# Row products with two weight matrices: from plain matmuls on row tiles to Strassen's scheme on pairs of row tiles

## The chip, the cores and the metric

The kernel runs on one core of a Trainium2 chip. The metric is device time in microseconds (us) of one execution, the median of several runs. A core has five engines with instruction streams of their own: TensorE (PE, matrix products; PEld its weight loads), VectorE (DVE), ScalarE (ACT), GpSimd (POOL) and SyncE (SP, which here only issues transfers). [...] 

## What is computed

Two layers of a graph network on 3327 nodes with D = 512 features, in float32:

```
# layer 0: attention; ahead of it a layer norm
h = relu(layernorm(x))
q, k, v = h @ Wq.T + bq, h @ Wk.T + bk, h @ Wv.T + bv
x1 = x + softmax(q @ k.T / sqrt(512) + adj + adj) @ v
# layer 1: normalised graph convolution
h1 = relu(layernorm(x1))
A2 = adj + I
dscale = diagonal(A2) ** -0.5
temp = A2 @ h1 @ W.T
out = x1 + relu((dscale * A2 * dscale) @ temp)      # dscale by rows and by columns
```

The kernel doesn't form v. With p for the exponentials it multiplies the square matrix with the rows of h first and with the weights after: (p @ h) @ Wv.T, divided by the sum of the row of p; the bias is then added to each row, since a row of the softmax sums to one. The same order is used in layer 1. So three times a square matrix of 26 x 26 row tiles (26 tiles of 128 rows, padded) meets rows of 512 numbers: p with h (g = 0), the adjacency with h1 (g = 1), and the adjacency with the rows that layer 1 made by the weights (g = 2). After g = 0 and after g = 1 each of the 26 row tiles is multiplied with a 512 x 512 weight matrix. These 52 row products are what is changed.

## The kernel before

**Prelude** (up to about 120 us of the trace): products of the weights, the layer norm and ReLU of x (`h_transposed`), transposes, and `project_q`. **Scores** (to about 640 us): `Pair` makes scores and their exponentials, and writes them to memory in the seven combinations that Strassen's scheme needs.

**Steps.** The three large products are done by Strassen's scheme with the 2 x 2 blocks of the matrix. There are 294 steps, numbered by `number_of(g, r, s, t)`: g is the product (0 to 2), r one of seven block products in the order p5, p1, p6, p7, p2, p3, p4, s one of two strips of columns (896 and 768 wide, so that a matmul has 448 or 384), and t runs over 0 to 5 and None. A step with t of 0 to 5 applies Strassen's scheme once more inside: `four_sums` (L170 to L172) makes three combinations of the left-hand tile on VectorE, `Right.make` four differences of the right-hand rows (L176 to L179), and seven matmuls (L772) add into seven PSUM banks (`ROLE`: p1 in bank 0, and so on). The step None has four matmuls (L764) for the thirteenth tile; its product p8 lies in bank 3. After it `gather` makes the strip's result from the banks: a copy of p1 on ScalarE (L796) and eight operations on VectorE (L797 to L805). `settle` (L820 to L827) adds it into the results of the 2 x 2 blocks: nothing for p5 and p1, six operations for p7, two for the others. The sums of step k + 2 are made behind the matmuls of step k, and its transfers are issued three steps ahead.

**Row products.** `times_weights` (L860) multiplies one row tile with a weight matrix by four matmuls of 512 columns into bank 3, the same that p8 and the transposes at the end use. In g = 0 `attend` then scales and adds x on VectorE (L872), adds the bias (L873), stores the tile (L874) and starts the norm (`norm`: L190, L192, L194 on VectorE, a power on GpSimd at L196, and nb on VectorE at L200); `attended`, one step later, applies the ReLU on ScalarE (L879) and stores the row (L880). x is loaded by ScalarE's queue one step ahead (L867). In g = 1 `temp` scales on ScalarE (L888) and stores. `rows` places one row tile beside a step, from the step (g, 5, 1, 2), where the first rows are complete, to the first strips of g + 1; a row tile's matmuls come behind those of its step. `Job` (L851, L854) makes sums of the adjacency for layer 1, in steps of g = 0 and g = 1.

**Order.** `run(k)` writes out the order in which each engine gets its work, and it is kept as written: the transfers of step k + 3, the matmuls of step k, the gather if t is None, the sums of step k + 2, settle, and then what `between` holds for this step (loads and blocks of the right-hand side, jobs, row products). In the third product `finish` (L913) transposes, applies ReLU, adds x1 and stores.

Of the kernel before, what the change touches and what calls it, by code (L numbers as in the profile page):

```python
# [10 lines left out]
F32 = mybir.dt.float32  # L11
# [29 lines left out]
Q = tuple(n * P // 2 for n in HT)  # L41


@with_exitstack
def graph_layers_kernel(
# [117 lines left out]
    totd = dram.tile([1, NP], F32, name="totd")  # L163
    x1d = [dram.tile([P, D], F32, name=f"x1d{i}") for i in range(NT)]
# [3 lines left out]
    def four_sums(o, g):  # L168

        nc.vector.tensor_add(o[:, 0:2], g[:, 0:4:3], g[:, 1:2].to_broadcast([P, 2, g.shape[-1]]))  # L170
        nc.vector.tensor_add(o[:, 2], o[:, 1], g[:, 0])  # L171
        nc.vector.tensor_add(o[:, 3], o[:, 2], g[:, 2])  # L172
# [93 lines left out]
    x_ring = ring(*((mid, k) for k in range(10, 15)), (half, 13), (half, 14))  # L266
    n_ring = ring(*((mid, k) for k in range(4)))

    def load_x(i, queue=nc.sync):
        xt = x_ring([P, D], "xt")  # L270
        queue.dma_start(xt, x[i * P : (i + 1) * P])
        return xt
# [16 lines left out]
    nc.sync.dma_start(bq_sb, bq)  # L289
    M = blocks(range(4, 8), "M")  # L290
# [3 lines left out]
    zero = half(12, [P, P], "zero")  # L294
# [16 lines left out]
    def h_transposed(k):  # L311

        a, n = PACKS[k]
        for _, i in (o for o in order if o[0] == k):
# [4 lines left out]
            nc.gpsimd.dma_start(rowd[0][i], ht)  # L319
# [11 lines left out]
        nc.vector.tensor_add(hp[k][:, 6], hp[k][:, 1], hp[k][:, 4])  # L331

    def project_q(k):
# [5 lines left out]
        def chain(o):  # L339
# [12 lines left out]
            def last():  # L352
                if o == 1:
                    for j in range(4):
                        y, z = divmod(j, 2)
                        i = (y * HALF + a) * P
                        nc.gpsimd.dma_start(qd[:, 2 * z : 2 * z + 2, i : i + w], qs[j][:, :, :w])
# [13 lines left out]
    for k, then in itertools.zip_longest(TURN, TURN[1:]):  # L371
        if then is not None:
            h_transposed(then)
        project_q(k)

# [30 lines left out]
    def adjacency(s, q, t):  # L406
# [3 lines left out]
        for k in range(2):  # L410
            r0, c0 = (k * HALF + t) * P, STRIPS[s] * P
            src = adjT[r0 : r0 + P, c0 : c0 + 2 * H[s]].rearrange("p (y w) -> p y w", y=2)
            nc.sync.dma_start(g[k], src[:, :, c : c + wd])
        return g

    class Pair:
# [11 lines left out]
        def sum_of_adjacency(self, m):  # L428
# [7 lines left out]
            for k, y in parts:  # L436
                d = diagonal(o, (k * HALF + t) * P, STRIPS[s] * P + y * H[s] + self.c)
# [138 lines left out]
    def seven():  # L576
        return {r: bank(ROLE[r], r) for r in ("p1", "p6", "p7", "p5", "p2", "p3", "p4")}
# [33 lines left out]
    rs = const.tile([P, NT], F32, name="rs")  # L611

    def weights(src):

        w = [half(k, [P, 2, D], "w") for k in (12, 13)]
        for c in range(DC):
            nc.sync.dma_start(w[c // 2][:, c % 2], src[c * P : (c + 1) * P])
        return [w[c // 2][:, c % 2] for c in range(DC)]
# [4 lines left out]
    bvs = []  # L623

    def prepare():
        wv_w1.append(weights(wvT))
        bvs.append(half(11, [P, D], "bv_sb"))
        nc.sync.dma_start(bvs[0], bass.AP(tensor=bv.tensor, offset=bv.offset, ap=[[0, P], [1, D]]))
# [4 lines left out]
    def prepared():  # L633
        nc.vector.reciprocal(rs, tot)
        nc.vector.tensor_scalar(dg, dg, 1.0, None, op0=ALU.add)
        nc.gpsimd.tensor_tensor(sd, dg, mh, op=ALU.pow)

    wv_w1 = []

    def other_weights():  # L640
        wv_w1.append(weights(w1T))
# [17 lines left out]
    r_ring = ring(*((half, k) for k in (4, 5, 6, 7)))  # L659
# [11 lines left out]
    job_ring = ring(*spare[2:], (half, 14))  # L671
    h_ring = ring(*spare[:2])
    ts_ring = ring(*spare[:3])
# [5 lines left out]
    def left(g, s, what, t):  # L679
# [4 lines left out]
        for k, j in enumerate(js):  # L684
# [7 lines left out]
            r0, c0 = (z * HALF + j) * P, STRIPS[s] * P + y * H[s]  # L692
# [6 lines left out]
    class Right:  # L699
# [9 lines left out]
        def rows(self, dst, h, z):  # L709

            for k, i in enumerate(self.its):
                src = rowd[self.g][h * HALF + i]
# [18 lines left out]
        def make(self):  # L731
            own, r = self.own, self.r
            if r == "p5":
                nc.vector.tensor_sub(own, self.two[:, :, 0:E], self.two[:, :, E:D])
            if r == "p6":
                nc.vector.tensor_add(own, own, self.two[:, :, 0:E])
                nc.vector.tensor_sub(own, own, self.two[:, :, E:D])
                nc.gpsimd.dma_start(self.t2[:, 0 : 2 * self.n], self.b[:, 0 : 2 * self.n])
            if r in ("p7", "p4"):
                nc.vector.tensor_sub(own, own, self.one)  # L740
            if self.n == 2:
                for _ in four_differences([self.b[:, k] for k in range(8)]):
                    pass

    class Step:
# [8 lines left out]
        def sums(self):  # L754
# [3 lines left out]
            four_sums(self.o, self.a.rearrange("p k y w -> p (k y) w"))  # L758

        def multiply(self, ps):  # L760
# [6 lines left out]
            o = self.o  # L767
            for r, i, m in (
                ("p1", 0, a[:, 0, 0]), ("p6", 5, o[:, 2]), ("p7", 6, o[:, 0]), ("p5", 4, o[:, 1]),
                ("p2", 2, a[:, 1, 0]), ("p3", 3, o[:, 3]), ("p4", 7, a[:, 1, 1]),  # L770
            ):
# [5 lines left out]
    def gather(ct, r, s, ps, last):  # L777

        hw, qw = H[s], Q[s]

        def region(y, z):
            return [ct[y][2 * z + k] for k in range(2)]

        place = {"p5": (1, 1), "p1": (0, 0)}.get(r)
        if place:
            to = region(*place)
        else:
            to = [cts["to"][k][:, :hw] for k in range(2)]
        p = {k: v[:, :qw] for k, v in ps.items()}
        lo, hi = slice(0, qw), slice(qw, hw)  # L790
        r11, r12, r21, r22 = region(0, 0), region(0, 1), region(1, 0), region(1, 1)
        into = r21 if last else None


        c11, c12, c21, c22 = to[0][:, lo], to[1][:, lo], to[0][:, hi], to[1][:, hi]
        nc.scalar.copy(c11, p["p1"])  # L796
        nc.vector.tensor_sub(c22, p["p6"], c11)  # L797
        nc.vector.tensor_add(c21, c22, p["p7"])
        nc.vector.tensor_sub(c12, c22, p["p5"])
        nc.vector.tensor_sub(c22, c21, p["p5"])  # L800
        if into is None:
# [4 lines left out]
        else:  # L806

            o11, o12, o21, o22 = (t[k][:, w] for t, k, w in ((into, 0, lo), (into, 1, lo), (into, 0, hi), (into, 1, hi)))
            nc.vector.tensor_add(o11, o11, c11)
            nc.vector.tensor_sub(o12, o12, c12)  # L810
            nc.vector.tensor_add(o21, o21, c21)
            nc.vector.tensor_add(o22, o22, c22)
            flags.append(nc.values_load(bad, min_val=0, max_val=1))
            for o, k in ((o11, "p2"), (o12, "p3"), (o21, "p4"), (o22, "p8")):
                nc.vector.tensor_add(o, o, p[k])

        def settle():
            for k in range(2):
                if r == "p6":
                    nc.vector.tensor_sub(r12[k], to[k], r11[k])  # L820
                elif r == "p7":
                    nc.vector.tensor_add(r21[k], to[k], r12[k])  # L822
                    nc.vector.tensor_sub(r12[k], r22[k], r12[k])  # L823
                    nc.vector.tensor_sub(r22[k], r21[k], r22[k])  # L824
                elif not place and into is None:
                    t = {"p2": r11, "p3": r12, "p4": r21}[r]
                    nc.vector.tensor_add(t[k], t[k], to[k])  # L827

        return settle
# [6 lines left out]
    class Job:  # L836
# [5 lines left out]
        def load(self):  # L842
            s, j, w = self.s, self.j, H[self.s]
            self.a, self.b = (job_ring([P, H[0]], "job")[:, :w] for _ in range(2))
            r0, c0 = (self.k * HALF + j) * P, STRIPS[s] * P
# [10 lines left out]
    def times_weights(i, w):  # L856
        s, y, k = where(i)
        ps = bank(ROLE["p8"], "p8")
        for d in range(DC):
            nc.tensor.matmul(ps, cts[s][y][d][:, k * P : (k + 1) * P], w[d], start=d == 0, stop=d == DC - 1)  # L860
        return ps

    xts = {}

    def attend_load(i):
        xts[i] = view(2, 1).rearrange("p a w -> p (a w)")[:, len(xts) % 3 * D :][:, :D]
        nc.scalar.dma_start(xts[i], x[i * P : (i + 1) * P])  # L867

    def attend(i):

        xt, ps = xts[i], times_weights(i, wv_w1[0])
        nc.vector.scalar_tensor_tensor(xt, ps, rs[:, i : i + 1], xt, op0=ALU.mult, op1=ALU.add)  # L872
        nc.vector.tensor_add(xt, xt, bvs[0])  # L873
        nc.gpsimd.dma_start(x1d[i], xt)  # L874
        normed[i] = norm(xt)

    def attended(i):
        h1 = h_ring([P, D], "h1")
        nc.scalar.activation(h1, xts[i], AF.Relu, bias=normed[i][1](), scale=normed[i][0])  # L879
        nc.gpsimd.dma_start(rowd[1][i], h1)  # L880

    normed = {}

    def temp(i):

        ps = times_weights(i, wv_w1[1])
        ts = ts_ring([P, D], "ts")
        nc.scalar.mul(ts, ps, sd[:, i : i + 1])  # L888
        nc.gpsimd.dma_start(rowd[2][i], ts)
# [62 lines left out]
    def rows(g, k, i, *z):  # L952

        if g == 0:
            at(k - 1, attend_load, i)
            at(k, attend, i)
            at(k + 1, attended, i)
        elif g == 1:
            at(k, temp, i)
        else:  # L960
            at(k - 1, finish_load, i, *z)
            at(k, finish, i, *z)


    for g in range(2):
        for t, i in {2: 0, 3: 1, 4: 2, 5: 3}.items():
            rows(g, number_of(g, 5, 1, t), i)
        for t, i in enumerate((4, 5, 6, 14, 15, 16)):
            rows(g, number_of(g, 6, 0, t), i)
        for t, its in {1: (7,), 2: (8, 9), 3: (10,), 4: (11, 12), 5: (13,)}.items():  # L970
            for i in its:
                rows(g, number_of(g, 6, 1, t), i)
# [431 lines left out]
```

## Time and profile before

| what | us |
|---|---|
| median of 3 runs (lowest, highest) | 2236.4 (2235.24, 2238.02) |
| the profiled execution | 2233.93 |
| its span, from the first to the last instruction | 2231.7 |
| TensorE busy | 2185.5 |
| VectorE busy | 1623.9 |
| ScalarE, GpSimd busy | 230.7, 354.8 |
| matmuls of steps: L772, L764 | 1255.5, 124.2 |
| matmuls of scores: L449, three kinds | 309.2, 162.6, 81.1 |
| row products: L860, two kinds of operands (272 and 144 records) | 125.5, 67.6 |

The program's matmuls of float32 stand in the trace as two records each, so that a row product has eight records of 512 columns. A matmul's end is modelled, so a record's duration is longer than the distance to the next one; distances between starts are what counts for TensorE. In the lists of waits a line says which engine and line waited for which, with the sum, the number of times and the longest. In a timeline each line has the start, the duration, the engine, the line, the operation with output and input, and in brackets how long the engine had been idle and what released it.

### The profile page before, as it was taken

How to read it: one execution, taken by the hardware profiler on the slowest of the kernel's cores; microseconds unless marked ns; L12 is line 12 of the kernel's file. 1: busy time of each engine (PE TensorE's matmuls, PEld its weight loads, DVE VectorE, ACT ScalarE, POOL GpSimd, SP SyncE). 2: the span in 40 equal slices, each digit the busy share in tenths (PEclk: the TensorE clock that was granted, in tenths of full speed). 3: DMA queues.
4: the chain of work that ended last, by engine and by line, in shares of the span. 5: the costliest groups of instructions: out<-in, count | busy, mean ns of one | idle time of the engine just before them, and what ended most of it. 6: DMA issues, size and time to landing. Idle time of an engine off the chain costs nothing. (4 is left out here: it accounts for less than half of the span.)

```text
span 2231.7 us, 21005 instructions
## 1 busy us (share of the span) xinstructions
PE 2185.5 (98%) x6268; PEld 1169.3 (52%) x6268; DVE 1623.9 (73%) x3092; ACT 230.7 (10%) x336; POOL 354.8 (16%) x551
## 2 busy tenths in 40 slices
PE   9999999999999999999999999999999999999997
PEld 5555555455545555555444555555544555555554
DVE  6369888788878788877777778886543547777676
ACT  5321121112110000000010000000000000000011
POOL 4223333333321000001221110000000000000001
PEclk9999999999999999999999999999999999999998
DMA  7568888888969998888787899876645458765695
GB/s 253 204 210 309 294 296 287 302 283 305 350 215 329 327 366 283 280 300 272 258 293 240 298 337 355 280 280 202 217 126 195 141 174 299 243 187 185 210 307 172
DMA packets 246682, 583.68 MB, mean 262 GB/s; under 512 B 34768, under 2 KB 106270, under 8 KB 246558
## 3 DMA queue, kind: packets, MB, share of 16 engines
q1 hardware_dynamic: 192270, 399.28, 54.2%
q0 software_dynamic: 44928, 167.49, 19.7%
q10 hardware_dynamic: 9360, 15.47, 2.2%
q8 instruction: 52, 0.85, 0.2%
q14 instruction: 72, 0.59, 0.1%
HBM read 414.28 MB, written 167.85 MB: 261 GB/s over the span
## 5 line engine op out<-in xcount | busy, mean ns | idle before, releaser
L772 PE MATMUL p<-part,b 128*128 128x448 f32 (+1 forms) x3528 | 1255.5, 514 | 5.2 <-DVE part L171 4.9
L772 PEld LDWEIGHTS p<-part,b 128*128 128x128 f32 x3528 | 669.2, 191 | 570.6 <-issue 302.5
L170 DVE TENSOR_TENSOR part<-part 128x896 f32<-128x896 f32 (+1 forms) x252 | 257.0, 1020 | 84.1 <-PE p L772 38.6
L449 PE MATMUL Y<-qt,hp 128*128 128x448 f32 (+1 forms) x832 | 309.2, 514 | 3.9 <-DVE g L453 2.7
L449 PEld LDWEIGHTS Y<-qt,hp 128*128 128x128 f32 x832 | 157.3, 190 | 139.5 <-issue 72.2
L449 PE MATMUL Z<-qt,hp 128*128 128x384 f32 (+1 forms) x416 | 162.6, 513 | 0.0
L172 DVE TENSOR_TENSOR part<-part,part 128x448 f32<-128x448 f32 (+1 forms) x219 | 129.5, 591 | 17.0 <-PE p L772 0.9
L171 DVE TENSOR_TENSOR part<-part,part 128x448 f32<-128x448 f32 (+1 forms) x219 | 129.5, 591 | 7.4
L860 PE MATMUL p<-w,ct 128*128 128x512 f32 x272 | 125.5, 601 | 5.8 <-DVE part L872 4.2
L764 PE MATMUL p<-part,b 128*128 128x448 f32 (+1 forms) x336 | 124.2, 513 | 0.0
L449 PEld LDWEIGHTS Z<-qt,hp 128*128 128x128 f32 x416 | 78.9, 190 | 67.3 <-issue 36.2
L453 DVE SCALAR_TENSOR_TENSOR g<-g,Y 128x384 f32<-128x384 f32 (+1 forms) x156 | 91.6, 587 | 26.9 <-PE Y L449 24.4
L854 POOL DMA_DIRECT2D sum<-job x52 | 28.4, 547 | 488.4 <-DVE job L851 272.9
L797 DVE TENSOR_TENSOR part<-p,part 128x384 f32<-128x384 f32 (+1 forms) x33 | 19.3, 586 | 106.0 <-ACT part L796 57.7
L764 PEld LDWEIGHTS p<-part,b 128*128 128x128 f32 x336 | 63.7, 190 | 53.9 <-issue 33.2
L860 PEld LDWEIGHTS p<-w,ct 128*128 128x128 f32 x272 | 51.9, 192 | 67.7 <-issue 51.9
L796 ACT COPY part<-p 128x384 f32<-128x384 f32 (+1 forms) x33 | 16.5, 499 | 669.1 <-PE p L772 669.1
L449 PE MATMUL X<-qt,hp 128*128 128x384 f32 (+1 forms) x208 | 81.1, 513 | 0.0
L456 ACT ACTIVATE g<-g 128x768 f32<-128x768 f32 (+1 forms) x48 | 43.0, 896 | 352.8 <-DVE g L453 291.8
L860 PE MATMUL p<-w,part 128*128 128x512 f32 x144 | 67.6, 606 | 7.2 <-DVE ct L805 4.8
L441 POOL DMA_DIRECT2D sum<-o x52 | 36.8, 708 | 220.5 <-DVE o L435 156.1
L872 DVE SCALAR_TENSOR_TENSOR part<-p,rs,part 128x512 f32<-128x512 f32 x26 | 19.5, 750 | 64.7 <-PE p L860 56.5
(165 smaller groups left out, 1875.8 us busy)
## 6 DMA issues: line engine op xcount, KB each, us to landing
part<-sum SPq DMA_DIRECT2D x104, 448.0 KB, 5.0
part<-p SPq DMA_DIRECT2D x91, 448.0 KB, 6.4
part<-sum SPq DMA_DIRECT2D x104, 384.0 KB, 3.5
part<-p SPq DMA_DIRECT2D x91, 384.0 KB, 4.1
part<-in_adjT_dram SPq DMA_DIRECT2D x78, 448.0 KB, 4.7
b<-row SPq DMA_DIRECT2D x234, 128.0 KB, 4.9
part<-in_adjT_dram SPq DMA_DIRECT2D x78, 384.0 KB, 3.8
g<-in_adjT_dram SPq DMA_DIRECT2D x52, 448.0 KB, 4.6
```

The lines of the kernel that those rows point to most:

```text
L170: nc.vector.tensor_add(o[:, 0:2], g[:, 0:4:3], g[:, 1:2].to_broadcast([P, 2, g.shape[-1]]))
L171: nc.vector.tensor_add(o[:, 2], o[:, 1], g[:, 0])
L172: nc.vector.tensor_add(o[:, 3], o[:, 2], g[:, 2])
L441: nc.gpsimd.dma_start(self.to(sumd)[:, 0:2], self.o)
L449: nc.tensor.matmul(ps[:, :wd], h_of(self.t, name, k), qt[B[name]][:, k], start=start and k == 0, stop=k == 1, skip_group_check=True)
L453: nc.vector.scalar_tensor_tensor(a[n], a[n], 2.0, ps[:, :wd], op0=ALU.mult, op1=ALU.add if sign > 0 else ALU.subtract)
L456: nc.scalar.activation(g[1], g[1], AF.Exp, **({"bias": pad} if self.t == HALF - 1 else {}))
L764: yield nc.tensor.matmul(ps[("p2", "p3", "p4", "p8")[k]][:, :w], b[:, z], a[:, 0, y], start=k == 3, stop=True)
L772: yield nc.tensor.matmul(ps[r][:, :w], b[:, i], m, start=self.t == 0, stop=self.t == PAIRS - 1 and r in ("p1", "p5", "p6", "p7"))
L854: nc.gpsimd.dma_start(sumd[self.s][self.j][:, 2 + self.k], self.a)
L860: nc.tensor.matmul(ps, cts[s][y][d][:, k * P : (k + 1) * P], w[d], start=d == 0, stop=d == DC - 1)
L872: nc.vector.scalar_tensor_tensor(xt, ps, rs[:, i : i + 1], xt, op0=ALU.mult, op1=ALU.add)
```

## The change

It has four parts.

1. **Row products on pairs.** `Weighted` (with `Attended` for g = 0 and `Temp` for g = 1) multiplies two row tiles at a time with the weight matrix by seven products of half the width and half the depth: two matmuls of 256 columns each. They are set between the matmuls of two steps, at the places in `AFTER`. All seven use the two halves of bank 3 ("pw"). p2, p5, p6 and p4 are read by ScalarE, m1, p3 and p7 by VectorE. Eight additions of 128 columns (`sums`) per pair, on VectorE, make the combined row tiles at the end of the step ahead of the pair. The weights' combinations are made in eight VectorE operations and two on ScalarE. x plus the bias is made in the prelude (`biased`: 26 additions and 26 stores), and an accumulating transfer (`close`) adds it to the row tile in place of the load of x and the two additions. `norm` stands at the end of the step two after the pair's first, the ReLU and its store (`then`, now in place) at the opening of the step three after. Where a step holds products, VectorE's tasks are written out two per matmul instead of all behind it.
2. **The gather in two parts.** `first` (the copy and four operations) comes after the step t = 5, behind its first three tasks; `rest` (four operations) and `settle` come after the step None, behind three tasks, which are the sums of a later step.
3. **Bank 3 for rows only.** p8 goes to the bank of p1, and a step with t = 0 multiplies p1 last.
4. **Another order of row tiles.** `ROW` permutes the row tiles, so that the upper halves of both strips come first.

The rings of small buffers move with it: the ring of row tiles for the right-hand side has three slots in place of four. The core of the diff:

```diff
+ROW = tuple(STRIPS[s] + y * HT[s] + k for y in range(2) for s in range(2) for k in range(HT[s]))
...
+    def biased(k):
+        for _, i in (o for o in order if o[0] == k):
+            xt = loaded.pop(i)
+            nc.vector.tensor_add(xt, xt, bv_sb)
+            nc.gpsimd.dma_start(xbd[ROW[i]], xt)
...
-    r_ring = ring(*((half, k) for k in (4, 5, 6, 7)))
+    r_ring = ring(*((half, k) for k in (4, 5, 6)))
...
+            for r, i, m in seven + first if self.t == 0 else first + seven:
...
-    def times_weights(i, w):
-        s, y, k = where(i)
-        ps = bank(ROLE["p8"], "p8")
-        for d in range(DC):
-            nc.tensor.matmul(ps, cts[s][y][d][:, k * P : (k + 1) * P], w[d], start=d == 0, stop=d == DC - 1)
-        return ps
...
+    PARTS = (("p2", 1, True, 0, 1), ("m1", 0, True, 0, -1), ("p5", 1, False, 3, -1), ("p6", 0, False, 1, -1),
+             ("p3", 1, False, 1, 1), ("p7", 0, False, 3, 1), ("p4", 0, False, 2, 1))
+    class Weighted:
...
+        def multiply(self, j):
+            name, k, new, _, _ = PARTS[j]
+            left = {"m1": 0, "p2": 1, "p4": 3}.get(name)
+            for c in range(2):
+                a = self.o[:, {"p7": 0, "p5": 1, "p6": 2, "p3": 3}[name], c] if left is None else self.blocks[left][c]
+                nc.tensor.matmul(self.ps[:, k], a, W[B[name]][:, c], start=new and c == 0, stop=c == 1,
+                                 skip_group_check=True)
+        def read(self, j):
+            name, k, _, n, sign = PARTS[j]
+            i = self.its[n // 2]
+            to, ps = self.to[n // 2][:, n % 2 * E : (n % 2 + 1) * E], self.ps[:, k]
+            scale = self.scales[sign][:, i : i + 1]
+            if name in ("p2", "p5", "p6", "p4"):
+                nc.scalar.mul(to, ps, scale)
+            else:
+                nc.vector.scalar_tensor_tensor(to, ps, scale, to, op0=ALU.mult, op1=ALU.add)
...
+    class Attended(Weighted):
...
+        def close(self):
+            for i, xt in zip(self.its, self.to):
+                nc.gpsimd.dma_start(xt, xbd[i], accum_op=ALU.add)
+        def norm(self):
+            self.normed = []
+            for i, xt in zip(self.its, self.to):
+                nc.gpsimd.dma_start(x1d[i], xt)
+                self.normed.append(norm(xt))
+        def then(self):
+            for i, xt, (rstd, bias) in zip(self.its, self.to, self.normed):
+                nc.scalar.activation(xt, xt, AF.Relu, bias=bias(), scale=rstd)
+                nc.gpsimd.dma_start(rowd[1][i], xt)
...
+    AFTER = ((0, 0), (0, 2), (0, 4), (0, 6), (1, 1), (1, 3), (1, 5))
+    def pair(g, k, *its):
+        w = (Attended, Temp)[g](*its)
+        coming.setdefault(k - 1, []).append((w.sums, ()))
+        for j, (n, m) in enumerate(AFTER):
+            inserted.setdefault((k + n, m), []).append((w, j))
+        if g == 0:
+            coming.setdefault(k + 2, []).insert(0, (w.norm, ()))
+            opening[k + 3] = w.then
...
+            (0, 5, 1, 2): (0, 1), (0, 5, 1, 4): (2, 3),
+            (0, 6, 0, 0): (4, 5), (0, 6, 0, 2): (6, 14), (0, 6, 0, 4): (15, 16),
+            (0, 6, 1, 0): (17, 18), (0, 6, 1, 2): (19, 7), (0, 6, 1, 4): (8, 9),
+            (1, 0, 0, 0): (10, 11), (1, 0, 0, 2): (12, 13), (1, 0, 0, 4): (20, 21),
+            (1, 0, 1, 0): (22, 23), (1, 0, 1, 2): (24, 25),
...
     def run(k):
...
-            banks_of["p8"] = bank(ROLE["p8"], "p8")
-        for j, _ in enumerate(step.multiply(banks_of)):
+            banks_of["p8"] = bank(ROLE["p1"], "p8")
...
+        sums = steps[k + 2].sums() if k + 2 < len(steps) else ()
+        tasks = itertools.chain(sums, flow(between.get(k, ())))
+        weighs = any((k, j) in inserted for j in range(7))
+        if k in opening:
+            opening[k]()
+        for j, _ in enumerate(itertools.chain((None,), step.multiply(banks_of))):
+            for w, n in inserted.get((k, j), ()):
+                w.product(n)
...
+            for _ in itertools.islice(tasks, 2 if weighs and j else 0):
+                pass
+        if t == PAIRS - 1 and not last:
+            for _ in itertools.islice(tasks, 3):
+                pass
+            gatherer.first(banks_of)
+        if t is None:
+            for _ in itertools.islice(tasks, 3):
+                pass
+            gatherer.rest(banks_of)
+            gatherer.settle()
+        for _ in itertools.chain(tasks, flow(coming.get(k, ()))):
+            pass
```

## The prediction

> **What bounds the kernel now.** First the page's busy shares: TensorE works 98% of the span, so only what shortens or interrupts its stream counts.
>
> ```profile
> PE 2185.5 (98%) x6268; PEld 1169.3 (52%) x6268; DVE 1623.9 (73%) x3092; ACT 230.7 (10%) x336; POOL 354.8 (16%) x551
> ```
>
> Then the waits of the whole run, TensorE's lines (total us, times, longest), which say how little it is interrupted:
>
> ```profile
> PE p L772 <- DVE part L171: 4.9, 4, 1.9
> PE p L860 <- DVE ct L805: 4.8, 2, 4.0
> PE p L860 <- DVE part L872: 4.2, 3, 2.5
> PE pt L913 <- DVE part L824: 3.1, 2, 2.5
> ...
> PE p L860 <- DVE part L827: 2.5, 2, 1.8
> ...
> PE p L860 <- ACT ts L888: 1.7, 2, 0.8
> ```
>
> The weights products (L860) own 13.2 us of it, all in two windows, whose busy time follows (columns: span, then PE, PEld, DVE, ACT, POOL, clock, DMA):
>
> ```profile
> 1035.00:1265.00 230.00, 219.75 (x575) 109.17 (x574) 165.30 (x331) 19.04 (x27) 50.50 (x76) 0.99 0.79 270
> 1640.00:1805.00 165.00, 161.93 (x437) 82.38 (x436) 71.42 (x135) 13.30 (x21) 8.77 (x17) 1.00 0.54 167
> ```
>
> In the first VectorE is 72% busy, in the second 43%. The timeline of TensorE prices a pass: from one start to the next, eight 512-column records take 3.44 us (430 ns each), fourteen of 448 5.26 (376), fourteen of 384 4.51 (322).
>
> ```profile
> 1074.63 3.60 PE L860 MATMUL p<-w,ct 128*128 128x512 f32 x8
> 1078.07 5.43 PE L772 MATMUL p<-part,b 128*128 128x448 f32 x14
> 1083.33 1.88 PE L860 MATMUL p<-w,ct 128*128 128x512 f32 x4
> ...
> 1672.54 4.68 PE L772 MATMUL p<-part,b 128*128 128x384 f32 x14
> 1677.05 3.60 PE L860 MATMUL p<-w,ct 128*128 128x512 f32 x8
> ```
>
> Last the timeline at the largest stall, a strip's end; ScalarE, then VectorE, then TensorE:
>
> ```profile
> 1209.25 0.81 ACT L879 ACTIVATE h<-part,nb,rstd 128x512 f32<-128x512 f32 x1 [8.31 <-DVE nb L200]
> ...
> 1209.97 0.51 ACT L796 COPY ct<-p 128x448 f32<-128x448 f32 x1
> ```
>
> ```profile
> 1210.52 0.62 DVE L797 TENSOR_TENSOR ct<-p,ct 128x448 f32<-128x448 f32 x1 [1.35 <-ACT ct L796]
> ...
> 1214.56 0.61 DVE L805 TENSOR_TENSOR ct<-ct,p 128x448 f32<-128x448 f32 x1
> ...
> 1215.09 0.95 DVE L170 TENSOR_TENSOR part<-part 128x768 f32<-128x768 f32 x1
> ```
>
> ```profile
> 1208.01 3.17 PE L764 MATMUL p<-part,b 128*128 128x448 f32 x8
> 1215.23 2.08 PE L860 MATMUL p<-w,part 128*128 128x512 f32 x2 [4.05 <-DVE ct L805]
> ```
>
> A ReLU that waits for VectorE's nb holds the copy on ScalarE, the copy holds the gather, the gather holds a weights product that wants its bank. After 4.05 us of idling two 512-column records take 2.08 us, not 0.86: the stall also costs clock.
>
> [...] stalls of 2 us and more in this trace are followed by about 3.4 us at 0.5, a loss of 1.7 us. [...]
>
> **The change part by part, on the profiled execution (2233.9; span 2231.7).**
> *Columns.* 26 row tiles x 2 groups x 8 records x 429 ns = 178.5 us go. 26 pairs x 7 products x 4 records of 256 columns come; from the three paces [...] a record is an estimated 216 ns, so 157.0 us. Weight loads stay hidden: they are 190 ns each, and transposes of 128 columns already run at 109 ns. **-21.5.** A product is 0.86 us; a step's matmul (two records) 0.75 or 0.64.
>
> *The single bank.* In the changed kernel's instruction lists each product waits for the read of the product before it, though that lies in the other half: m1 for p2's read on ScalarE, p5 for m1's on VectorE, p6 and p3 for ScalarE, p7 and p4 for VectorE. Only two step matmuls (1.3 to 1.5 us) lie between products. So a read that is queued late stops TensorE, where before a whole step lay between.
>
> *Strip ends, first window.* There are four within runs of pairs: A, B, C behind strips that settle, D behind p5, which settles nothing. From the end of the last p4 of a strip, ScalarE reads it (0.45, estimate from the 448-column copy at 0.51) and copies c11 (0.5). Then VectorE has, at A, by start-to-start times of before's timeline: four gather operations 2.1, sums 2.3, the other four 1.9, settle 2.0, right-hand blocks 1.6 (512 columns 0.65, four differences 0.93), norm of two row tiles 2.05, eight row sums of 128 columns 1.75 (0.22 each, as L176 to L179), nb 0.15: 13.85. The new pair's first read, on ScalarE, is queued behind the old pair's two ReLUs (2 x 0.81), which wait for nb: 1.0 + 13.85 + 1.6 + 0.45 = 16.9. TensorE wants m1 after two matmuls 1.3, the None step 2.6, p2 0.86, two matmuls 1.5: 6.2. Stall 10.7. B, with 448 widths and a job: 10.2; C 10.7; D, without settle and blocks, 6.9. Sum 38.5, plus 4 x 1.7 of clock: 45.3. Before, this window lost 16.1 (its three waits of 10.0, the clock and short gaps). **+29.** With c11 not delayed and durations 10% shorter it would be +20; with the product order intact it can't be nothing.
>
> *Strip ends, second window.* No norm, no ReLU; m1's read on VectorE stands behind gather, settle, blocks, row sums and two sums operations: at A 1.0 + 2.1 + 2.3 + 1.9 + 2.0 + 1.6 + 1.75 + 1.65 + 0.42 = 14.7, and p5 is wanted at 6.2 + 0.86 + 1.5 = 8.6: 6.1. B 4.6, C 6.1, D 2.5: 19.3, plus 6.8 of clock, less 4.2 lost before. **+22**; low end +8, when stalls stay too short for the clock and D vanishes.
>
> *Within strips.* p3's and p7's reads share VectorE with sums and blocks, two per matmul: 0.1 to 0.4 late a pair. **+3** (0 to 8).
>
> *Accumulates.* 52 ScalarE loads and VectorE adds (26 x 0.69 us, off the path) become 26 GpSimd accumulates of 256 KB, unseen before. The norm waits for two of them, in VectorE's order before p3's read, and p7 waits for that. Between p4's end and p7 lie 12.0 to 13.3 us; read 0.5, two issues 1.2, norm with pow 3.0 and read 0.4 leave 6.9 (384) or 8.2 us (448) for landing. Stores and loads of that size land in a median 3.8 to 5.4 us here. I take them hidden: **0**; if they need 10, five pairs lose 3.1 and four 1.8, +23.
>
> *Prelude.* 26 VectorE adds (about 0.6) and 26 GpSimd stores (0.55 issue) lie where VectorE has 41.6 of the first 65 us busy. TensorE is full from 65 us on, which hides most. **+2** (-2 to +8). The weights' differences (8 VectorE operations, 2 on ScalarE) sit in steps with slack: 0.
>
> *Gather in two, bank 3 for rows, row order.* Sums now run ahead of the last four gather operations and settle, about 2 us earlier: of the stalls outside the windows (L171, L824 and their clock loss at 880, 915, 1439, 1472, 1985 and 2012 us) I take 10 of some 13 away, and 1 at the tail. **-11** (-13 to -3). p8 in p1's bank waits for the copy, done 1.0 us after p4, before TensorE reaches it.
>
> *Queues and rings.* The bias load moves from SP to ScalarE's queue in the prelude; 26 loads of x leave ScalarE's queue; GpSimd keeps its x1d and row stores and gets the accumulates ahead of them, so a pow behind them waits for their issue (in the 3.0 above). The ring of row tiles for right-hand blocks shrinks from four slots to three: SP's loads behind a block's load would be late if a slot weren't free, but a row load lands in 4.9 us and is made use of two steps on, over 10 us: 0.
>
> Sum: -21.5 + 29 + 22 + 3 + 0 + 2 - 11 = +23.5: 2257.4, and with the median 2.5 above the profiled execution 2260.
>
> **Rivals.**
> 1. *The lists are short enough* (faster). If at strip ends the vector list is drained in time and the eight stalls are what before shows for most such places, 1.5 us each: 12 in place of 71.3 (45.3 and 26.1), so 2201. For it: 28% and 57% of VectorE's time is free in the windows, and in the scores stage finely mixed work at 81% VectorE left TensorE 99% busy. Against: the free time isn't at strip ends, where the list is 14 us against 6. It decides when a stall with its clock falls below 6.0 us on average (71.3 - 23.5 = 47.8 over eight).
> 2. *Half of it.* Stalls are real but only the first window's ReLU chain bites: 2235 to 2242, no change or just slower.
> 3. *The accumulates are late*: +23 on top, 2283; decided by the landing time of the 256 KB accumulate.
> That the columns don't fall is excluded: they are counted.
>
> **Chances.** Main case (2243 to 2275) 0.5; rival 1 with anything under 2232 0.24; rival 2 0.14; rival 3 or more 0.12. A measurement tells 0.2% (4.5 us) from no change: faster 0.24, same 0.07, slower 0.69. Range 2208 to 2286: it cuts a part of rival 1 and the far end of 3. The likeliest case's own range is 2243 to 2275.
>
> **What would show it.** L925 waiting for VectorE's and ScalarE's reads at eight strip ends, 7 to 11 us in the first window and 2 to 6 in the second, each with a clock dip; weights records near 216 ns; ReLU L963 on ScalarE idle for nb just before m1; no L171 or L824 stalls outside; accumulates landing under 7 us. I am wrong if the waits of L925 sum to under 30 us, or if the accumulate shows as VectorE's releaser.

## The result and the profile after

The changed kernel takes 2286.2 us (2285.23 to 2287.5), the one before 2235.8 in the same session: a ratio of 1.0227, 95% interval 1.0211 to 1.0242, or 50 us more. The direction and the place were as forecast. The size was not: the forecast was 2260, 24 us more than before. The profiled execution's span grew from 2231.7 to 2283.4 us.

The page of the changed kernel, busy shares: TensorE is busy 5 us less, and 95% of the span in place of 98%.

```profile
PE 2180.4 (95%) x6580; PEld 1236.7 (54%) x6580; DVE 1672.8 (73%) x3372; ACT 263.0 (12%) x417; POOL 383.7 (17%) x603
```

The waits of the whole run, TensorE's lines. L925 is the pairs' products, L935 their reads on ScalarE, L937 those on VectorE, L788 the matmuls of the step None, L824 the copy of p1, L358 `project_q`:

```profile
PE pw L925 <- ACT part L935: 43.8, 4, 14.0
PE pw L925 <- DVE ts L937: 20.1, 6, 6.2
PE Y L358 <- ACT qs L363: 6.0, 1, 6.0
PE p L788 <- ACT part L824: 5.2, 1, 5.2
PE tp L329 <- DVE nb L204: 3.1, 1, 3.1
...
PE p L796 <- DVE part L841: 2.8, 3, 1.9
```

The row products waited 13.2 us before and wait 65.5 us now. Four of those waits are for ScalarE, in the first window; four of the six for VectorE's ts are strip ends of the second. The windows (PE, PEld, DVE, ACT, POOL, clock, DMA, GB/s) show the clock too: it fell to 0.91 and 0.95.

```profile
1035.00:1300.00 265.00, 219.19 (x723) 141.25 (x723) 163.79 (x412) 42.36 (x75) 69.69 (x109) 0.91 0.75 234
1640.00:1860.00 220.00, 199.60 (x664) 129.06 (x663) 124.61 (x305) 22.93 (x49) 12.42 (x23) 0.95 0.45 147
```

The first strip end in the timeline, TensorE first: four records of 256 columns take 0.87 us from start to start (in the whole trace a record's usual distance is 216 ns, as estimated), and then m1 waits 14 us.

```profile
1050.48 1.03 PE L925 MATMUL pw<-w,ct 128*128 128x256 f32 x4
1051.35 1.67 PE L796 MATMUL p<-part,b 128*128 128x448 f32 x4
1067.00 2.07 PE L925 MATMUL pw<-w,ct 128*128 128x256 f32 x4 [13.99 <-ACT part L935]
```

What ScalarE does in that time: the first ReLU waits for VectorE's nb, the second for a transfer, and only then p2 is read.

```profile
1061.55 0.81 ACT L963 ACTIVATE part<-part,nb,rstd 128x512 f32<-128x512 f32 x1 [13.56 <-DVE nb L204]
1065.77 0.81 ACT L963 ACTIVATE w<-w,nb,rstd 128x512 f32<-128x512 f32 x1 [3.41 <-DMA x1d<-w]
1066.49 0.45 ACT L935 ACTIVATE part<-pw,rs 128x256 f32<-128x256 f32 x1
```

VectorE works without a gap from the gather's first operation, which the copy releases, to nb, 13.3 us later:

```profile
1048.03 0.56 DVE L825 TENSOR_TENSOR part<-p,part 128x384 f32<-128x384 f32 x1 [1.51 <-ACT part L824]
...
1054.33 1.82 DVE L857 TENSOR_TENSOR part<-part,part 128x768 f32<-128x768 f32 x2
...
1057.72 0.69 DVE L194 BATCH_NORM_STATS2 st<-part 128x6 f32<-128x512 f32 x1
...
1061.37 0.22 DVE L204 SCALAR_TENSOR_TENSOR nb<-mv,rstd 128x1 f32<-128x1 f32 x2
```

So the list of the prediction (13.85 us) stands there as written. What was not in it is the second ReLU's bracket: it writes its tile in place, and must wait until the store of that tile (x1d) has read it. Without that it would have started 0.72 us behind the first, as such pairs do elsewhere; so the store costs 3.5 us here.

Where the 51.7 us of the span went. For each stage, "lost" is TensorE's time over its streaming pace, worked out from the distances between matmul starts. The pace is 0.833 ns a column and 2.3 ns a record, a fit to the usual distances in the two traces: 109, 216, 376 and 429 ns for 128, 256, 448 and 512 columns. The first window's figures reach to 1265 us before and 1308 after, so that the last pair's stall is in it.

| stage | lost before | lost after | difference | forecast |
|---|---|---|---|---|
| columns of the row products | | | -21.5 | -21.5 |
| prelude | 15.2 | 24.2 | +9.0 | +2 |
| scores | 8.4 | 7.1 | -1.3 | 0 |
| first window | 16.3 | 63.8 | +47.5 | +29, and half of the 3 within strips |
| second window | 4.2 | 29.8 | +25.6 | +22, and the other half |
| other steps | 16.9 | 11.4 | -5.5 | -10 |
| behind the last matmul | | | -2.2 | -1 |

### The profile page after: what moved, and what is told of

Same layout as the page of the kernel before. It is cut to its first block, busy times and chain, and to the rows that moved or that the text cites. A ratio compares the mean times of both kernels' runs of the same rounds, so it can differ in the third digit from the quotient of the medians.

```text
span 2283.4 us, 22028 instructions
## 1 busy us (share of the span) xinstructions
PE 2180.4 (95%) x6580; PEld 1236.7 (54%) x6580; DVE 1672.8 (73%) x3372; ACT 263.0 (12%) x417; POOL 383.7 (17%) x603
## 5 line engine op out<-in xcount | busy, mean ns | idle before, releaser
L796 PE MATMUL p<-part,b 128*128 128x448 f32 (+1 forms) x3528 | 1282.9, 516 | 3.4 <-DVE part L841 2.8
L788 PE MATMUL p<-part,b 128*128 128x448 f32 (+1 forms) x336 | 125.2, 515 | 5.2 <-ACT part L824 5.2
L925 PE MATMUL pw<-w,rows 128*128 128x256 f32 x416 | 111.5, 392 | 19.3 <-DVE ts L937 19.1
L925 PEld LDWEIGHTS pw<-w,rows 128*128 128x128 f32 x416 | 81.9, 198 | 61.7 <-DVE ts L937 21.8
L470 DVE SCALAR_TENSOR_TENSOR g<-g,Y 128x384 f32<-128x384 f32 (+1 forms) x156 | 91.4, 586 | 29.1 <-PE Y L466 25.6
L788 PEld LDWEIGHTS p<-part,b 128*128 128x128 f32 x336 | 63.7, 191 | 58.0 <-issue 30.1
L925 PE MATMUL pw<-w,ct 128*128 128x256 f32 x192 | 53.5, 403 | 39.8 <-ACT part L935 36.7
L824 ACT COPY part<-p 128x384 f32<-128x384 f32 (+1 forms) x33 | 16.5, 501 | 634.0 <-PE p L796 633.2
L825 DVE TENSOR_TENSOR part<-p,part 128x384 f32<-128x384 f32 (+1 forms) x33 | 19.4, 587 | 73.9 <-PE p L796 60.1
L925 PEld LDWEIGHTS pw<-w,ct 128*128 128x128 f32 x192 | 36.9, 198 | 62.1 <-ACT part L935 38.8
```

The costliest lines, as they stand in the source:

```text
L470: nc.vector.scalar_tensor_tensor(a[n], a[n], 2.0, ps[:, :wd], op0=ALU.mult, op1=ALU.add if sign > 0 else ALU.subtract)
L788: yield nc.tensor.matmul(ps[("p2", "p3", "p4", "p8")[k]][:, :w], b[:, z], a[:, 0, y], start=k == 3, stop=True)
L796: yield nc.tensor.matmul(ps[r][:, :w], b[:, i], m, start=self.t == 0, stop=self.t == PAIRS - 1 and r in ("p1", "p5", "p6", "p7"))
L925: nc.tensor.matmul(self.ps[:, k], a, W[B[name]][:, c], start=new and c == 0, stop=c == 1, skip_group_check=True)
```

## The experiments

Two questions: do the reads' places in the queues set the strip ends' stalls, and what are the 28 us that the forecast missed?

### The prelude: x directly

```diff
         project_q(k)
-        biased(k)
...
-                nc.gpsimd.dma_start(xt, xbd[i], accum_op=ALU.add)
+                nc.gpsimd.dma_start(xt, x[i * P : (i + 1) * P], accum_op=ALU.add)
```

> The accumulating transfer takes x itself; x plus bias is not made in the prelude (the bias, which is zero in these inputs, is left out). Theory (the prelude lost 9 us in the changed kernel because the buffers of x come free only when the sum of x and bias has been stored, so that later loads on SP, of x, of the adjacency and of the queries, start late): the stalls of 3.1 us (tp behind nb, 55 us) and 6.0 us (Y behind the scaling of queries, 101 us) vanish, and the kernel gains 7 to 10 us, to 2276 to 2279. Rival (the prelude's loss comes from the other order of row tiles or from the loads' share of the transfer engines, whatever is stored): gain under 3 us. The row products after 1035 us are as in the changed kernel.

Measured: 2281.3 us, ratio 1.0216 (1.0199 to 1.0233); the prelude lost 15.2 us in its trace, as before the change. Both stalls are gone (under 1 us and 1.4 us are left in their places), and at 2263 us, where the last step ends, it is 7.1 us ahead. The timed gain, 5 us, or 2.5 beside the kernel before of its own session, is below the forecast one: the last stores ended some 3 us later behind the last matmul in this trace. The theory holds for the prelude as far as this run goes, which takes away the 26 additions and stores together with the waits; the timed gain is smaller than its interval can tell well. The waits of SP's queue in the changed kernel's first 125 us, with the longest two groups, say where the time goes:

```profile
SPq L275 <- DMA xb<-xt: 46.2, 13, 11.8
SPq L430 <- DMA xb<-xt: 13.0, 2, 10.7
```

L275 loads x, L430 the adjacency: both wait for a buffer that the store of x plus bias still reads. The sum of such waits is no measure by itself, for before the change SP's loads waited as long for other things (96 us in the same stretch, 84 now); what counts is when they start. The last of the 26 loads of x is issued at 65.2 us here, at 55.0 before the change and at 41.6 in this run; the load of queries that precedes the stall at 101 us is issued at 101.5, 93.9 and 93.7.

### The ReLUs behind the reads

```diff
-        if k in opening:
+        if k in opening and t != 0:
             opening[k]()
...                                        # behind the step's matmuls and reads
+        if k in opening and t == 0:
+            opening[k]()
```

> At strip ends the two ReLUs of the last pair are queued on ScalarE behind all reads of the step t = 0, not ahead of p2's read. Theory (m1 waits for p2's read, which is behind the ReLUs, which wait for VectorE's list and for the store of the row tile that they overwrite): the wait of L925 for ScalarE, 43.8 us in four stalls, vanishes; in its place p5 waits for m1's read on VectorE behind the same list, 4 to 8 us each, 26 to 32 in all; the kernel gains 12 to 18 us, to 2268 to 2274. Rival (VectorE's list alone sets the stall, and the ReLUs merely stand in it): p5 waits as long as m1 did, gain under 4 us.

Measured: 2273.8 us, ratio 1.0178 (1.0161 to 1.0195), 12.4 us below the changed kernel, or 10 when each is taken beside the kernel before of its own session. The four waits for ScalarE are gone, and p5 waits for m1's read instead, as forecast. The waits of this run, and the first strip end in its timeline:

```profile
PE pw L925 <- DVE part L937: 27.4, 4, 7.9
PE pw L925 <- DVE ts L937: 20.1, 6, 6.2
```

```profile
1066.40 2.07 PE L925 MATMUL pw<-w,rows 128*128 128x256 f32 x4 [7.86 <-DVE part L937]
```

In VectorE's list m1's read ends 0.06 us before that product begins. So of the waits in the first window VectorE's list alone makes 27 us, and the ReLUs ahead of p2's read another 16.

### The stores ahead of the powers

```diff
             for i, xt in zip(self.its, self.to):
                 nc.gpsimd.dma_start(x1d[i], xt)
-                self.normed.append(norm(xt))
+            for xt in self.to:
+                self.normed.append(norm(xt))
```

> GpSimd issues both stores of a pair's row tiles ahead of both powers, so that the second store starts some 2.5 us earlier where GpSimd waits for VectorE in between. Theory (the ReLU works in place and so waits until the store of its tile has read it; at the first strip end that adds 3.4 us to VectorE's list): the stall of 14.0 us shrinks to 11 to 12, the third (12.8) by 0 to 2, the others hardly; gain 2 to 5 us. Rival (the list alone): no change within 1.5 us.

Measured: 2287.1 us (ratio 1.0243, 1.0226 to 1.0261). The first strip end shrank from 14.0 to 10.9 us: the wait for the store was 3 us of it. Over all four the sum fell only from 43.8 to 41.0, and the time didn't fall at all: other stalls of that execution (the prelude, the scores) were longer. The mechanism shows at one place; as a gain it is a miss (2 to 5 us were expected).

### No accumulates

```diff
         def close(self):
-            for i, xt in zip(self.its, self.to):
-                nc.gpsimd.dma_start(xt, xbd[i], accum_op=ALU.add)
+            pass
```

> The 26 accumulating transfers are left out (x and bias are not added). Rival of the prediction (late accumulates hold VectorE at the norm, and through it the reads of p3 and p7, in every pair): gain of 20 us or more. Theory (they are hidden but for the last pair, where the norm waits 6.8 us, the ReLU is late, the copy of p1 stands behind it and p8, which has p1's bank, waits 5.2 us; elsewhere the list and the ReLU chain set the stalls): that one stall vanishes with its clock, and the four strip ends change by less than 2 us each; gain 5 to 12 us.

Measured: 2281.4 us (ratio 1.0214, 1.0197 to 1.0231). That is 5 us below the changed kernel, or 2 beside the kernel before of its own session, less than the 5 to 12 expected. The wait of L788 for the copy is gone; the strip ends stay, as the waits say:

```profile
PE pw L925 <- ACT part L935: 40.7, 4, 13.5
PE pw L925 <- DVE ts L937: 20.1, 6, 6.2
```

So the accumulates are not what held the pairs back. Three of the four strip ends changed by about half a us; the third fell from 12.8 to 10.1, more than the 2 us allowed for (the two runs above that keep the accumulates and this order have 11.5 and 12.2 there). In the changed kernel the accumulates land in a median 6.2 us (10.7 at most). VectorE's norm waits for them 14.8 us in eight places, and most of it doesn't reach TensorE. The last pair pays: its norm and its stores wait for them (6.8 us the norm), the ReLUs in place wait for the stores, the copy of p1 is queued behind the ReLUs, and p8, which now lies in p1's bank, waits 5.2 us. In the changed kernel's trace:

```profile
1305.66 0.81 ACT L963 ACTIVATE part<-part,nb,rstd 128x512 f32<-128x512 f32 x1 [1.94 <-DMA x1d<-part]
1306.38 0.46 ACT L824 COPY part<-p 128x384 f32<-128x384 f32 x1
1306.89 1.65 PE L788 MATMUL p<-part,b 128*128 128x384 f32 x2 [5.20 <-ACT part L824]
```

VectorE's nb for this ReLU had ended at 1301.4, so that some 4 us of the 5.2 are the store that the ReLU in place waits for.

### The other parts alone

Row products as before (one row tile, four matmuls of 512 columns, x loaded, bias added by VectorE), with the gather in two parts, bank 3 for rows, and the new order of row tiles.

> Row products as in the kernel before (one row tile a step, four matmuls of 512 columns, x loaded, bias added on VectorE), with the rest of the change kept: gather in two parts, p8 in the bank of p1, bank 3 for rows only, the new order of row tiles. Theory (the columns saved are real and the pairs' reads at strip ends cost more than three times that; the other parts gain what the sums ahead of settle give): no stall of TensorE over 3 us after 660 us, row products at 429 ns a record, and 5 to 12 us faster than the kernel before, 2222 to 2230. Rival (the other parts cost time themselves, for instance through p8's wait for the copy): at or above the time before.

Measured: 2219.9 us, ratio 0.9926 (0.9901 to 0.9952), against a kernel before of 2234.7. Here the last row tiles stood so late that three of them, by the order of the program, were multiplied after their input had been overwritten. The next kernel places them earlier:

> The plain row products with the rest of the change kept, once more, the last nine row tiles placed one a step behind the first strip of the next product. Theory (the other parts gain by themselves: the sums run ahead of settle, row products no longer share their bank with p8): within 4 us of the run of this kind before, 2216 to 2224. Rival (that run was fast only through where its last row tiles stood): 2230 or more.

Measured: 2221.4 us, ratio 0.9933 (0.9909 to 0.9957). The other parts gain 14 to 15 us by themselves, more than the 5 to 12 that I had expected: the two windows, which lost 20.5 us before, lose 12.2. Its longest waits of TensorE follow. The lines are numbered otherwise in this kernel: L788 is here the matmuls of the steps with t of 0 to 5, L833 the first operation of the gather's second part, L885 the row products:

```profile
PE p L788 <- DVE part L833: 8.4, 4, 4.0
...
PE p L885 <- DVE part L897: 1.7, 2, 0.8
PE p L885 <- ACT ts L913: 1.7, 2, 0.8
```

The longest group is the price of the divided gather: a step's p2 waits for the second part, which now stands behind three tasks. Row products wait only 3.4 us.

### The list taken apart

The core of the edit: what a pair that opens a strip needs goes ahead, and what it doesn't need goes behind its reads.

```diff
+        opens = t is None and (k + 1, 0) in inserted
...
         if t == PAIRS - 1 and not last:
             for _ in itertools.islice(tasks, 3):
                 pass
+            for _ in ahead[k].sums() if k in ahead else ():     # row sums of the pair at k + 2
+                pass
             gatherer.first(banks_of)
         if t is None:
             for _ in itertools.islice(tasks, 3):
                 pass
             gatherer.rest(banks_of)
+            if opens:                          # norm and blocks: in step k + 1, behind m1's read
+                late[k + 1] = [*coming.get(k, ()), *between.get(k, ())]
+                return                         # settle: in step k + 2, behind p3's read
             gatherer.settle()
```

> The changed kernel with VectorE's list at strip ends taken apart: the row sums of a pair that opens a strip stand ahead of the gather's first part, and settle, right-hand blocks and norm stand behind m1's read or in the step after; the ReLUs there stand behind the reads; the last pair's norm and ReLU come one step later, behind the copy of p1. No operation is left out. Theory (the eight stalls come from the place of the reads in VectorE's and ScalarE's queues, not from the amount of work): the waits of L925 fall from 65 us to under 10, the clock recovers, and the kernel takes 2200 to 2215. Rival (VectorE has too much to do around a strip's end, wherever it is put): stalls move to p3 and p7 or to the next pair and at least 30 us of waits of L925 remain, 2240 or more.

Measured: 2216.3 us, ratio 0.9909 (0.9877 to 0.9941). The waits of L925 are 14 us (under 10 were expected). This kernel leaves out the settle of one strip in the second group; the next has it:

> VectorE's list at strip ends taken apart, with every settle in its place: in the run of this kind before, the settle of one strip in the second group of row products (two additions of 896 columns, 2 us of VectorE) was missing. Theory: waits of L925 stay under 16 us, and the kernel takes 2212 to 2222, 15 to 22 us below the kernel before. Rival (that missing settle was what made room): 2230 or more.

Measured: 2214.5 us, ratio 0.9908 (0.9885 to 0.9931): 72 us below the changed kernel with the same operations. The waits of L925 are 12.5 us in place of 65.5, and TensorE's clock is back at a mean of 0.992:

```profile
PE pw L925 <- DVE ts L937: 5.9, 6, 2.7
...
PE pw L925 <- DVE part L937: 4.1, 5, 1.3
...
PE pw L925 <- DVE w L937: 2.5, 3, 1.1
```

VectorE's work is the same to 1.2 us (1671.6 and 1672.8): it was the order. Which of the moves gave how much, the row sums, settle, blocks, norm or the last pair, isn't shown: only the ReLUs have a run of their own. Nor was a second bank for the products tried; in this kernel seven banks hold a step's products, and bank 3 is theirs.

Beside the plain row products (2221.4) this is a gain of only 7 us, though 21.5 us of columns went: the prelude loses 25.9 us in place of 15.5, the windows 21.0 in place of 12.2.

### The prelude's price

Three ways to be rid of it, on top of the list taken apart. GpSimd adds the bias behind the accumulate of x (this kernel leaves out the same settle as the first of its kind):

```diff
+                nc.gpsimd.tensor_tensor(xt, xt, bvs[0], op=ALU.add)
                 nc.gpsimd.dma_start(x1d[i], xt)
```

> As the run with VectorE's list taken apart, and also: the accumulating transfer takes x itself, and GpSimd adds the bias to each row tile after it has landed (26 additions of 512 columns), both stores issued ahead of the powers. Theory (prelude's wait for stored sums costs about 7 us, GpSimd is idle enough to add): 5 to 8 us below that run, 2193 to 2208. Rival (GpSimd's additions make the norm late and with it p3's read): at or above that run.

Measured: 2226.5 us (ratio 0.9961, 0.9947 to 0.9974), 10 us slower than without it. The rival holds: in the group view an addition takes 1.38 us on average, and in the waits of the first window VectorE's norm waits 19.4 us for it. The prelude did gain, 10 us in the trace (15.1 us lost, 25.1 without this change), but the first window lost 27.3 in place of 10.8.

```profile
L959 POOL TENSOR_TENSOR part<-part,bv_sb 128x512 f32<-128x512 f32 x20 | 27.7, 1384 | 34.9 <-DMA part<-in_x_dram 34.7
```

```profile
DVE st L194 <- POOL part L959: 14.7, 6, 4.2
...
DVE st L194 <- POOL w L959: 4.7, 4, 1.4
```

The same addition on VectorE (`nc.vector.tensor_add` in its place):

> As the run in which the accumulating transfer takes x itself, but VectorE adds the bias (26 operations of 0.69 us) ahead of the norm, in place of GpSimd. Theory (GpSimd's additions of 512 columns made norms late there, and with them p3's and m1's reads): the stalls in the first window, 22.7 us there, fall under 14, and the kernel is 8 to 18 us faster than that run, 2208 to 2219. Rival (VectorE has no room for 1.4 us more a pair): within 4 us of that run, 2222 or more.

Measured: 2215.1 us (ratio 0.9911, 0.9888 to 0.9934): 11 us better than on GpSimd (this kernel also has the settle), and no better than the sums in the prelude. Beside the run with the sums there the prelude gains 13 us in the trace, and the first window loses 8. TensorE's waits for reads in the first window are 11.5 us, with GpSimd's additions 17.4.

The sums stay in the prelude, but each is made two row tiles behind its norm:

```diff
             loaded[i] = xt
+            if len(loaded) > 2:
+                biased(next(iter(loaded)))          # one row tile, in place of a pack
```

> As the run with VectorE's list taken apart, and in the prelude each sum of x and bias is made and stored two row tiles after its norm, in place of after the products of its pack, so that buffers of x come free sooner. Theory (the prelude loses 9 us because loads wait for buffers that late stores hold): the stall of 6 us at 101 us and that of 3 to 4 us at 55 us shrink, 4 to 9 us below the run without it. Rival (VectorE and GpSimd are full between 20 and 65 us, so that earlier additions stall the transposes): no gain, or a loss of up to 5 us.

Measured: 2209.3 us, ratio 0.9879 (0.9855 to 0.9903): 5 us below the run without it (their intervals overlap), 26 below the kernel before, 77 below the changed kernel. The stall at 101 us fell from 5.5 to 3.2; the one of 3.8 at 55 us became one of 3.1 at 61, where a transpose waits for its ReLU. The last load of x is issued at 55.3 us, in place of 65.3. So the theory is borne out for a third of the prelude's loss (22.6 us, in place of 25.9, and 15.2 before the change); the work of the sums, which stays, is a rival for the rest. The two profiled spans differ by 2.3 us only. Of the kernels here this is the fastest with every operation in place.

## Why the prediction was right and wrong

- **Columns** (-21.5): right, -21.5. A record of 256 columns takes 216 ns.
- **The single bank, and the lists at strip ends**: right as a mechanism and nearly in size. The four stalls in the first window were forecast as 10.7, 10.2, 10.7 and 6.9 and measured 14.0, 10.0, 12.8 and 7.1; those in the second as 6.1, 4.6, 6.1 and 2.5, and measured, as distances over the streaming pace, 6.4, 4.9, 6.0 and 2.5. Taking the lists apart without taking an operation away gave 72 us back. In the second window the clock's loss, 6.9 us, meets the forecast 6.8 by chance: three stalls cost 1.5 to 2.8, the fourth nothing.
- **The step that failed: strip ends, first window (+29, and half of +3; +47.5 measured, 17 more).** Three things were missing in its sum. First, the ReLU in place: I let it wait for nb alone, though the edit puts it into the tile that x1d's store still reads. In the trace this is 3.5, 0.4, 1.1 and 0.5 us at the four strip ends (the first ReLU's start behind its nb, and the second's behind the first, over what both take where no store is in the way); the run with the stores ahead shows the first, and for the others no run was made. At the third, VectorE also waits 0.6 for an accumulate and the copy is 0.5 late. All four stalls are 6.0 us over the forecast 38.5 (44.5 as distances over the pace). Second, the last pair: its chain accumulate, store, ReLU, copy, p8 costs 5.4 us with no pair behind it, and 2.5 of clock. I had cleared p8's wait for the copy by looking at the copy's time when nothing stood before it on ScalarE. The run without accumulates shows this one. Third, the clock: behind the four strip ends it was 0.50 for 5.9, 4.6, 4.5 and 3.1 us, which costs half of that, 9.1 us and not 4 x 1.7 = 6.8. (The 1.7 is half of the 3.4 us at 0.50 that begin within 0.9 us of the end of each of four stalls in the trace before, at 883, 1064, 1215 and 2016 us; that other stalls would cost the same was the author's estimate.) 6.0 + 7.9 + 2.3 make 16.2 of the 17.
- **Within strips** (+3): right. Away from the eight strip ends the waits of L925 sum to 2.6 us.
- **Prelude** (+2; +9.0): mis-sized. I counted VectorE's additions and GpSimd's issues, but not that a store which reads a buffer of x keeps it from the next load: here the added store moved the time at which the buffer came free (13 loads of x waited 46.2 us for it, up to 11.8), and the last load of x on SP came at 65.2 us in place of 55.0. The upper end of my bounds was +8. The run with x itself puts the loss back to 15.2; how much of it is the buffers and how much the work of the sums is open beyond the third that the earlier sums gave back.
- **Accumulates** (0): right for most pairs. They land in 6.2 us at the median; I had allowed 6.9 to 8.2. But the sign that I had named for being wrong did show: in the first window they are VectorE's releaser for 13.6 us in six waits. TensorE pays at the last pair and, by the run without them, up to 2.6 us at the third strip end.
- **Other parts** (-11): -9 by the table with all of it (-1.3, -5.5 and -2.2). The other steps gave 5.5 and not 10: at 2068 us the transposes of the last product still stall 2.3 us, and at 2198 us a stall of 2.0 us is new, where a step waits for the gather's second part (L841). Alone, without the pairs, they gain 14 to 15, some 8 of it in the windows, where the plain row products no longer wait for p8's gather (no such wait is in that run's list); in the changed kernel this gain can't be told from the pairs' losses.
- **Rivals**: the first (lists short enough) is excluded for this order of work, and is what the kernel becomes when the lists are taken apart: 2214, where I gave it 2201. The second, that only the ReLU chain bites, is excluded by the second window. The third, late accumulates, is excluded as the main cause by the run without them.
- **The range** ended at 2286.0; the terms that it was built from had their upper ends at +8 for the prelude and nothing for the ReLUs and the last pair.

## What to carry to other kernels

Here products went through one PSUM bank, and the place of their reads in the engines' queues set what they cost: TensorE's products waited 65.5 us for them in one order and 12.5 in another, with the same operations. In such a case write down what stands ahead of it at the busiest point, not on average, and move behind it whatever the next product doesn't need. Making the ReLU work in place added 3.5 us at the first strip end, and with a further store that reads the buffers of x the last load of x came 10 us later: in an edit of either kind ask which transfer still reads that buffer, and what is queued behind the instruction that then waits. The parts of a change should be tried one by one: here the gather, the bank and the row order alone were worth 14 us, hidden under some 50 us of new waits.

## What was not expected of the hardware

In these two traces how long the clock stayed down behind a stall didn't follow the stall's length. In the changed kernel the granted clock was 0.50 for 5.9, 4.6, 4.5 and 3.1 us behind stalls of 14.2, 10.2, 12.9 and 7.3 us, and for 3.0, 5.2 and 5.6 us behind stalls of 6.4, 4.9 and 6.0. Behind four stalls of 2.0 to 2.7 us there was no such dip, though in the kernel before a stall of 2.1 us, at 881 us, was followed by 3.4 us at 0.50. An addition of 512 columns took a median 1.28 us on GpSimd, in the run where it adds the bias, and 0.69 on VectorE, in the kernel before. In the changed kernel a float32 accumulate of 256 KB into SBUF landed in a median 6.2 us, where the groups of plain stores of the same size from the same queue landed in 3.0 to 4.7.
